# One mixed count tile, and one bias product instead of two, in a graph layer on one core

## The chip, the cores and the metric

The kernel runs on one core of a Trainium2 chip. The core has a matrix engine (PE, with its weight load shown apart as PEld), a vector engine (DVE), a scalar engine (ACT), a general engine (POOL) that also issues the indirect gathers, and a queue engine (SP) that issues most DMAs. [...] The metric is device time of one launch in microseconds (us), lower is better.

## The reference

One layer of a graph network with 12,500 nodes of 128 features and 400,000 edges sorted by target node. Each edge has a type, 0 or 1.

```python
Xs = X[src]
m_data = Xs @ W_data.T + b_data
m_ctrl = Xs @ W_control.T + b_control
msg = jnp.where((edge_types == 0)[:, None], m_data, m_ctrl)
agg = jax.ops.segment_sum(msg, dst, num_segments=X.shape[0])
out = agg + (X @ W_self.T + b_self)
x = _layernorm(x + jax.nn.relu(out), axis=-1)
```

Sums and products can be exchanged: for each node the source rows of its type-0 edges and of its type-1 edges are summed first, and the two sums are then multiplied with the two weight matrices. The bias of a type enters as often as the node has edges of that type, so the kernel also counts edges by type, and the biases are added as (count of type 0) x b_data + (count of type 1) x b_control + b_self.

## The kernel before, in words

**Work and windows.** The edges are cut into 25 groups (`NG`) of 500 target nodes each (`GN`). A group is worked in 4 or 5 windows; there are 107 windows (`pairs`), and the loop over `w` near the end of `short_path` writes one after the other. In a window most source rows come from a copy of the node table kept in SBUF (`x3`): one-hot matrices choose rows with PE (`pick`, L820), ACT casts the result from PSUM to bf16 (`emsg`, L834), and PE multiplies that with one-hot matrices of the target nodes (`sums`, L704), which DVE makes by comparing (`esel`, L504). Other rows are gathered from DRAM by POOL (L754). DVE also ranks the edges of later windows in the table (L504 to L690).

**Accumulators.** `sums` is added by DVE into `acc[g]` (L743), a tile of 128 partitions x 4 x 640 in f32, whose last axis runs over nodes. Parts 0 and 1 hold the two feature sums, transposed. Parts 2 and 3 hold the counts of type 0 and type 1. Counts come from PE products with `one_col` (L790, L842), whose first six columns are 1 and the others 0: so the same count lands on partitions 0 to 5 of parts 2 and 3 (and in the other quarters of 32 partitions, L842 adds the counts of three quarters of its chunks on 32 to 37, 64 to 69 and 96 to 101).

**Biases in bf16.** A bias is split into three bf16 parts whose sum is the f32 value (`bparts`, L414). Those nine rows go to DRAM (`b_parts`, one DMA, L422), and from there into the tile `bias` (`bias_rows`, L427): partitions 0 to 2 and 3 to 5 of each quarter carry the three parts of b_data (part 0 of `bias`) and of b_control (part 1). Partitions 6 to 8 of part 0 carry b_self, with a count of 1 put there from the start by `start1` (L319).

**Finishing.** When a group is complete, `finish_batch` (L911) handles up to four tiles of up to 125 nodes; there are 26 such batches with 101 tiles. Its units are `begin` (load of x), `counts`, `turn` (transpose x), one `product` a tile, `norm` and `write`. `counts` makes `cnt`, in bf16, for both types at once: ACT casts the two count parts, 128 x 1000 elements, to bf16 (L928); DVE then computes `cnt * left + acc` over the same elements (L929), where `left` is -1 on partitions 3 to 5 of a quarter and 0 elsewhere. So partitions 0 to 2 hold the rounded count and 3 to 5 what rounding left of it. `product` (L941) adds into one PSUM tile: x with the self weights, the two feature sums with their weights (these three in f32, two PE instructions each), and two bf16 products, `cnt` with `bias` for type 0 and for type 1. That is eight PE instructions a tile, all on L950.

**Order.** The units of a finished group are the list `rest` and are laid evenly over the part from 0.1 to 1 of the next window (`evenly(rest, 0.1)`, `merged`): `pass_on`, the finishing units, `begin_acc`. This is the written order; the framework then lays out each engine's order itself from the written order, the dependencies and its own estimate of durations, and sets the semaphore waits. The last group is split into two batches: the last one's `counts` is held back as `cnt2` and runs after the last accumulation, at the end of the kernel, followed by its products, `norm` and `write` (L1085, L1107).

The diff touches `short_path` with its inner functions `bparts`, `bias_rows` and `finish_batch`.

Of the kernel before, what the change touches and what calls it, by code (L numbers as in the profile page):

```python
# [17 lines left out]
P = 128  # L18
D = 128
# [4 lines left out]
NG = NC // GC  # L24
# [5 lines left out]
NE = 5  # L30
# [10 lines left out]
CAP = 32  # L41
# [109 lines left out]
def short_path(ctx, tc, const, ident, eps, wT, brow, bad, x, src, dst, etype, ws, bs, out):  # L151
    nc = tc.nc
    keep = ctx.enter_context(tc.tile_pool(name="keep", bufs=1))
    dram = ctx.enter_context(tc.tile_pool(name="dram", bufs=1, space=DRAM))
# [74 lines left out]
    for kind, i, c, _ in windows(0):  # L229
        if kind == "p":  # L230
            n = PL if i == NE - 1 else PB
            nc.sync.dma_start(
                out=near_i[i * PB:i * PB + n, :],
                in_=dst.rearrange("(o g e) -> o g e", o=1, g=NG)[:, :, c * P].to_broadcast([n, NG]),
# [49 lines left out]
    split_units, store_rows = split_x(pro.enter_context(tc.tile_pool(name="pro", bufs=4)))  # L284
    tmp = early.enter_context(tc.tile_pool(name="tmp", bufs=1))
    wn = tmp.tile([P, 3, D], FP, name="wn")
    bias = keep.tile([P, 2, D], BF, name="bias")
    nc.vector.memset(bias, 0.0)
    for i, (w, b) in enumerate(zip(ws, bs)):
        nc.sync.dma_start(out=wn[:, i, :], in_=w)  # L290
# [22 lines left out]
    lane_f = keep.tile([P, 1], FP, name="lane_f")  # L313
    nc.vector.tensor_copy(lane_f, iota([1], [[0, 1]], 0, 1, "i3"))
    zero = keep.tile([P, 1], FP, name="zero")
# [1 line left out]


    start1 = keep.tile([P, 1], FP, name="start1")  # L319
    nc.vector.tensor_scalar(start1, lane_f, 7.0, None, op0=OP.subtract)  # L320
    nc.vector.tensor_tensor(start1, start1, start1, op=OP.mult)
    nc.vector.tensor_single_scalar(start1, start1, 1.0, op=OP.is_le)
    left = keep.tile([P, 1], FP, name="left")
    quarter_i = iota([1], [[0, 1]], 0, 1, "i8")
    nc.vector.tensor_single_scalar(quarter_i, quarter_i, CAP - 1, op=OP.bitwise_and)
    nc.vector.tensor_scalar(left, quarter_i, 4.0, None, op0=OP.subtract)
    nc.vector.tensor_tensor(left, left, left, op=OP.mult)
    nc.vector.tensor_scalar(left, left, 1.0, -1.0, op0=OP.is_le, op1=OP.mult)
    blks = [keep.tile([P, NE, 2 * EC], BF, name=f"blk{k}") for k in range(3)]
    for t in blks:  # L330
        nc.vector.memset(t, -1.0)
# [13 lines left out]
        nc.vector.tensor_scalar(ltri[:, a, :], free[:, a, :], own_f[:, a:a + 1], None, op0=OP.is_gt)  # L345
    one_col = keep.tile([P, P], BF, name="one_col")
    nc.vector.memset(one_col, 0.0)
    nc.vector.memset(one_col[:, 0:6], 1.0)
    scale = tmp.tile([1, 2, P], BF, name="scale")
    nc.vector.memset(scale[:, 0, :], 128.0)  # L350
    nc.vector.memset(scale[:, 1, :], 1.0)
# [57 lines left out]
            nc.tensor.transpose(wps[:, i * D:(i + 1) * D], wn[:, i, :], ident)  # L409
        nc.scalar.copy(wT, wps[:, :3 * D].rearrange("p (i d) -> p i d", d=D))  # L410

    b_parts = dram.tile([3, 3, D], BF, name="b_parts")

    def bparts():  # L414

        part = tmp.tile([1, 3, 3, D], BF, name="part")
        rest = tmp.tile([1, 3, D], FP, name="rest")
        nc.vector.tensor_copy(part[:, 0], brow)
        nc.vector.tensor_tensor(rest, brow, part[:, 0], op=OP.subtract)
        nc.vector.tensor_copy(part[:, 1], rest)  # L420
        nc.vector.tensor_tensor(part[:, 2], rest, part[:, 1], op=OP.subtract)
        nc.sync.dma_start(  # L422
            out=b_parts.rearrange("j i d -> (j i d)").rearrange("(o e) -> o e", o=1),
            in_=part.rearrange("o j i d -> o (j i d)"),
        )

    def bias_rows():  # L427
        for at in [at + k for at in range(0, P, CAP) for k in (0, 3)]:
            nc.sync.dma_start(out=bias[at:at + 3, :, :], in_=b_parts[:, 0:2, :])
        nc.sync.dma_start(out=bias[6:9, 0, :], in_=b_parts[:, 2, :])  # L430


    codes = {}
# [468 lines left out]
    def finish(g, ks):  # L902
        full = P - 3
        tiles = []
        for k in ks:
            a, b = min(k * full, GN), min(k * full + full, GN + M0)
            a = M0 if g == 0 and k == 0 else a
            tiles.append((g * GN - M0 + a, a, b - a))
        return finish_batch(g, tiles)

    def finish_batch(g, tiles):  # L911
        s = {}
# [3 lines left out]
        def begin():  # L916
# [4 lines left out]
            for i, (n, _, rows) in enumerate(tiles):  # L921
                nc.sync.dma_start(out=s["xs"][:rows, i, :], in_=x[n:n + rows, :])

        def counts():
            a, b = tiles[0][1], tiles[-1][1] + tiles[-1][2]
            cnt = fp.tile([P, 2, 512], BF, name="cnt", bufs=1)
            s["cnt"] = cnt[:, :, :b - a]
            nc.scalar.copy(s["cnt"], acc[g][:, 2:4, a:b])  # L928
            nc.vector.scalar_tensor_tensor(  # L929
                s["cnt"], s["cnt"], left, acc[g][:, 2:4, a:b], op0=OP.mult, op1=OP.add  # L930
            )

        def turn():
            ps = side()
# [6 lines left out]
        def product(i):  # L941
            if i == 0:
                s["ph"] = side()
            _, c, rows = tiles[i]
            terms = [(s["xT"][:, i * P:i * P + rows], wT[:, 2, :])]
            terms += [(acc[g][:, t, c:c + rows], wT[:, t, :]) for t in range(2)]
            at = c - tiles[0][1]
            terms += [(s["cnt"][:, t, at:at + rows], bias[:, t, :]) for t in range(2)]
            for j, (left, right) in enumerate(terms):
                nc.tensor.matmul(  # L950
                    s["ph"][:rows, i * D:(i + 1) * D], left, right, start=(j == 0), stop=(j == len(terms) - 1)
                )
# [29 lines left out]
                )  # L982
                nc.sync.dma_start(out=out[n:n + r, :], in_=h[:r, i, :])

        return [begin, counts, turn] + [lambda i=i: product(i) for i in range(k)] + [norm, write]


    pairs = len(each_e)
# [77 lines left out]
    for w in range(pairs):  # L1066
        g, i = each_e[w]
        more = []
        if i == 1 and g + 1 < NG:
            more.append((0.1, lambda: prep_e(g + 1)))  # L1070
        if i == 1 and g + 1 < NG:
            more += evenly(prep_p(g + 1), 0.1, 0.7)
        if i == 3 and g + 2 < NG:
            load(g + 2, "e")
            load(g + 2, "p")
        tiled, begin = {}, []
        if w + 2 < pairs:
            tiled, begin = slots[w + 2]["tiled"], begun.pop(w + 2)
        elif w + 2 == pairs:
            tiled, begin = last_spares()  # L1080
        if w + 3 < pairs:
            more += [(0.55, lambda: [u() for u in begin_slots(w + 3)])]
        if w + 1 == pairs:
            closes = [at for at, _ in chunks[w]][-1 - of_p(NG - 1, NE - 1)]
            (xs, *most), (xs2, cnt2, turn2, *last) = (finish(NG - 1, soon[i]) for i in (NE - 2, NE - 1))  # L1085
            more += [(0.05, xs), (0.06, xs2), (0.98, turn2), (0.3, check_all)] + evenly(most, closes + 0.01, 0.97)
        units, ending = picked(w, tiled, ending, begin.pop(0)[1] if begin else None)
        merged(
            chunks.pop(w, []),
            units,  # L1090
            begin,
            pick_matrix(w + 1) if w + 1 < pairs else [],
            more,
            evenly(rest, 0.1),
        )
        slots.pop(w)
        rest = []
        for p in closed.pop(w, []):
            gp, ip = divmod(p, NE)
            if ip == NE - 1:  # L1100
                rest.append(lambda gp=gp: pass_on(gp))
                if gp < NG - 1:
                    rest += finish(gp, range(4))
                if gp + 2 < NG:
                    rest.append(lambda gp=gp: begin_acc(gp + 2))
    ending()
    for u in rest + [cnt2] + last:  # L1107
        u()


# [138 lines left out]
```

## Time and profile before

| | before |
|---|---|
| median of 3 runs | 1758.43 us (1756.07 to 1759.98) |
| the profiled execution, its own time | 1757.87 us |
| span of the profiled execution | 1756.1 us |
| PE busy in the span | 1615.3 us |
| DVE busy in the span | 1595.2 us |
| ACT busy in the span | 1229.2 us |
| POOL busy in the span | 1316.6 us |

How to read the views. A group row gives line, engine, operation, the written tile and what it reads, the shapes and the count; then busy time in us and the mean of one instruction in ns; then the idle time of that engine just before these instructions, with what ended most of it. The chain of waits is the work that ended last, followed back: a piece on it had nothing earlier to wait behind, and a piece off it had room. A timeline row is start, duration, engine, line, operation; in brackets stands an idle time before it and who ended it; "x2" means two merged instructions. Instructions of DVE and ACT overlap a little at their ends, so the distance from start to start is shorter than a duration. A piece marked "issue" is time in which the profile shows no wait. In the windows table each engine's busy time in a stretch stands with its number of instructions in brackets.

### The profile page before, as it was taken

To read this page: it belongs to the slowest core of one execution; us is meant where nothing else is said; L and a number is where in the kernel's file an instruction comes from. 1 tells how busy PE (TensorE), PEld (TensorE's weight loads), DVE (VectorE), ACT (ScalarE), POOL (GpSimd) and SP (SyncE) were. 2 spreads that over 40 slices of the span, in tenths; PEclk is the share of its full clock that TensorE was granted. 3 is DMA by queue.
4 is the path that set the end of the run, shared out by engine and by line. 5 is a ranking of instruction groups with operands and counts; after the bars stand their busy time and mean duration, and the time that the engine had idled before them with its cause. 6 is when DMAs were issued, how large, how long until landed. Compare 5 with 4: busy or idle time off the path is not lost.

```text
span 1756.1 us, 72083 instructions
## 1 busy us (share of the span) xinstructions
PE 1615.3 (92%) x29945; PEld 1311.7 (75%) x29945; DVE 1595.2 (91%) x3996; ACT 1229.2 (70%) x2249; POOL 1316.6 (75%) x1109
## 2 busy tenths in 40 slices
PE   0599999999999999999999999999999989999997
PEld 0377777777778777777877877777777777878786
DVE  8899999998999998999988999999999989999993
ACT  4577777767677667767766777776777766767675
POOL 0288877787777787877887877887877877777871
PEclk9999999999999999999999999999999999999999
DMA  8655454446454545444535454544454535544441
GB/s 237 209 165 160 128 158 136 147 125 199 115 164 134 159 125 179 143 152 127 166 119 164 150 164 133 164 122 147 160 159 135 158 108 162 167 139 141 151 139 41
DMA packets 190562, 261.28 MB, mean 149 GB/s; under 512 B 86437, under 2 KB 155983, under 8 KB 187152
## 3 DMA queue, kind: packets, MB, share of 16 engines
q1 hardware_dynamic: 126894, 148.02, 25.9%
q0 software_dynamic: 50704, 102.16, 20.8%
q10 hardware_dynamic: 12626, 6.40, 1.2%
q8 instruction: 236, 3.87, 0.9%
q14 instruction: 102, 0.84, 0.1%
HBM read 238.47 MB, written 18.00 MB: 146 GB/s over the span
## 4 chain that ended last, share of the span: by engine, by line
PE 48%; DVE 32%; issue 6%; DMA 6%; ACT 5%; DVEq 1%; POOL 1%; SPq 0%; POOLq 0%; ACTq 0%
PE sums L704 22%; PE got L820 15%; DVE esel L504 3%; PE side L950 3%; DVE pick L690 3%; PE sums L842 3%; DMA last<-rows,idx 3%; DVE rv L635 2%; ACT emsg L834 2%; DVE prod L598 2%; DVE prod L576 2%; PE side L584 2%; DVE acc L743 2%; PE side L647 2%; DVE ahead L594 2%
## 5 line engine op out<-in xcount | busy, mean ns | idle before, releaser
L754 POOL DMA_INDIRECT msg<-rows,pidx x985 | 1190.9, 1209 | 307.5 <-issue 118.9
L834 ACT CAST emsg<-got 128x768 bf16<-128x768 f32 (+1 forms) x1070 | 951.9, 930 | 303.9 <-PE got L820 289.8
L704 PE MATMUL sums<-esel,emsg 128*128 128x176 bf16 x7704 | 683.4, 240 | 0.0
L704 PEld LDWEIGHTS <-emsg 128*128 128x128 bf16 x7704 | 566.9, 98 | 68.7 <-issue 28.5
L820 PE MATMUL got<-x,pick 128*32 128x384 bf16 x10486 | 568.0, 330 | 21.9 <-DVE pick L690 14.7
L820 PEld LDWEIGHTS <-pick 128*32 128x32 bf16 x10486 | 239.2, 96 | 139.2 <-issue 20.6
L504 DVE TENSOR_TENSOR esel<-code_col,code 128x1760 bf16<-128x1760 bf16 x321 | 292.7, 912 | 13.6 <-PE sums L704 11.6
L798 POOL DMA_INDIRECT last<-rows,idx x107 | 122.0, 1141 | 106.0 <-DVE pick L690 63.7
L704 PE MATMUL sums<-psel,msg 128*128 128x48 bf16 x2955 | 184.2, 184 | 17.2 <-DVE acc L743 15.2
L842 PE MATMUL sums<-esel,one_col 128*32 128x176 bf16 x2675 | 193.7, 240 | 4.4 <-DVE acc L743 4.4
L704 PEld LDWEIGHTS <-msg 128*128 128x128 bf16 x2955 | 149.9, 97 | 36.2 <-issue 31.4
L842 PEld LDWEIGHTS <-one_col 128*32 128x32 bf16 x2675 | 111.9, 97 | 60.7 <-issue 4.1
L790 PE MATMUL sums<-psel,one_col 128*128 128x48 bf16 x985 | 150.2, 183 | 0.0
L743 DVE TENSOR_TENSOR acc<-acc,sums 128x352 f32 (+2 forms) x232 | 99.4, 430 | 40.4 <-PE sums L704 36.8
L504 DVE TENSOR_TENSOR O<-cell_col,blk 128x2000 bf16<-128x2000 bf16 x107 | 128.2, 1198 | 2.1 <-issue 2.1
L598 DVE TENSOR_TENSOR prod<-O,ahead 128x2000 bf16<-128x2000 bf16 x107 | 127.6, 1193 | 0.1
L690 DVE TENSOR_SCALAR pick<-pick,lane_f 128x3200 bf16<-128x3200 bf16 x107 | 113.2, 1058 | 0.0
L647 PE MATMUL side<-rv,O 128*128 128x64 bf16 x2140 | 83.3, 195 | 31.6 <-DVE rv L635 30.6
L647 PEld LDWEIGHTS <-O 128*128 128x128 bf16 x2140 | 78.7, 100 | 33.3 <-DVE rv L635 29.3
L594 DVE TENSOR_REDUCE ahead<-side 128x100 bf16<-128x500 f32 x107 | 72.2, 675 | 28.0 <-PE side L520 27.3
L790 PEld LDWEIGHTS <-one_col 128*128 128x128 bf16 x985 | 94.3, 96 | 0.0
L635 DVE TENSOR_TENSOR rv<-rm,vals 128x1280 bf16<-128x1280 bf16 x107 | 87.8, 821 | 0.3
(170 smaller groups left out, 1869.2 us busy)
## 6 DMA issues: line engine op xcount, KB each, us to landing
pick<-there SPq DMA_DIRECT2D x107, 800.0 KB
acc<-acc_start SPq DMA_DIRECT2D x23, 1280.0 KB
msg<-rows,pidx POOLq DMA_INDIRECT x985
rows<-x SPq DMA_DIRECT2D x6, 1344.0 KB
xs<-in_x_dram SPq DMA_DIRECT2D x99, 62.5 KB
out_dram<-h SPq DMA_DIRECT2D x99, 62.5 KB
xt<-in_x_dram ACTq DMA_DIRECT2D x6, 896.0 KB
there<-cell SPq DMA_DIRECT2D x107, 6.2 KB
```

What stands on the lines that cost most here:

```text
L504: nc.vector.tensor_tensor(sel.rearrange("p n (w t) -> p n w t", t=2), col[:rows].rearrange("p (o w t) -> p o w t", o=1, t=2).to_broadcast( ...
L598: nc.vector.tensor_tensor(prod, s["O"], ahead.rearrange("p (o j) -> p o j", o=1).to_broadcast([P, EC, NCELL]), op=OP.mult)
L635: placed[:] = [nc.vector.tensor_tensor(rv.rearrange("p c v (r t) -> p c v r t", t=2), rm.rearrange("p c (o r t) -> p c o r t", o=1, t=2).t ...
L647: nc.tensor.matmul(s["rk"][:m, :2 * CAP], s["held"][:, c * NCELL:c * NCELL + m], s["rv"][:, c].rearrange("p v r -> p (v r)"), start=(c == ...
L690: nc.vector.tensor_scalar(t, t, lane_f, None, op0=OP.is_equal)
L704: last = nc.tensor.matmul(out, msg[:, j * D:(j + 1) * D], sel, start=(start and j == 0), stop=stop, skip_group_check=True)
L743: added.append(nc.vector.tensor_add(win, win, ps[:, :4 * wide].rearrange("p (a w) -> p a w", w=wide)[:, :, :width]))
L754: return nc.gpsimd.indirect_dma_start(out=msg, out_offset=None, in_=rows3[:, :], in_offset=bass.IndirectOffsetOnAxis(ap=codes["p", g][0][: ...
L790: nc.tensor.matmul(cnt, one_col, sel, start=False, stop=(c == n - 1), skip_group_check=True)
L820: last = nc.tensor.matmul(ps[CAP * a:CAP * (a + 1), :], slots[w]["pick"][:, a * NQ + q, :], x3[:, 4 * q + a - a0].rearrange("p j d -> p (j ...
L834: nc.scalar.copy(msg[:, :n], ps[:, :n, :3 * D])
L842: nc.tensor.matmul(cells_of(s["ps"], EW, 1)[CAP * (q % 4):CAP * (q % 4 + 1), :], one_col[:, :CAP], s["sel"][q], start=(q < 4), stop=(q + 4 ...
```

## The change

Type 1's counts move to partitions of their own, so that one tile holds both types.

- `one_col` has twelve ones instead of six: each count lands on partitions 0 to 11 of a quarter.
- Four small [128, 1] tables replace one: `left` is now -1 on partitions 3 to 5 and 9 to 11, `second` is 1 on partitions 6 to 11, `plain` is 1 - `second`. `start1` moves to partitions 12 to 14.
- `bias` has one part instead of two: three parts of b_data on partitions 0 to 2 and 3 to 5, of b_control on 6 to 8 and 9 to 11, of b_self on 12 to 14 of the first quarter. `b_parts` is written in that order by five DMAs instead of one, and `bias` is read by four instead of nine.
- A new unit `mixed` comes before `counts`: ACT computes `mix = second * (counts of type 1)` in f32, 128 x 500, and DVE adds `plain * (counts of type 0)` to it. `counts` then does what it did, on `mix`: 128 x 500 instead of 128 x 1000 elements in both instructions.
- `product` has one bf16 product a tile in place of two.
- The held-back unit at the end becomes two, `mix2` and `cnt2`. The list `rest` has one unit more, so all its units stand a little elsewhere in the window.

```diff
-    bias = keep.tile([P, 2, D], BF, name="bias")
+    bias = keep.tile([P, D], BF, name="bias")
...
-    nc.vector.tensor_scalar(start1, lane_f, 7.0, None, op0=OP.subtract)
+    nc.vector.tensor_scalar(start1, lane_f, 13.0, None, op0=OP.subtract)
...
-    nc.vector.tensor_scalar(left, quarter_i, 4.0, None, op0=OP.subtract)
-    nc.vector.tensor_tensor(left, left, left, op=OP.mult)
-    nc.vector.tensor_scalar(left, left, 1.0, -1.0, op0=OP.is_le, op1=OP.mult)
+    kinds = [left] + [keep.tile([P, 1], FP, name=name) for name in ("left2", "second", "plain")]
+    for t, mid, wide in zip(kinds, (4.0, 10.0, 8.5), (1.5, 1.5, 7.0)):
+        nc.vector.tensor_scalar(t, quarter_i, mid, None, op0=OP.subtract)
+        nc.vector.tensor_tensor(t, t, t, op=OP.mult)
+        nc.vector.tensor_scalar(t, t, wide, -1.0 if t is not kinds[2] else 1.0, op0=OP.is_le, op1=OP.mult)
+    _, left2, second, plain = kinds
+    nc.vector.tensor_add(left, left, left2)
+    nc.vector.tensor_scalar(plain, second, -1.0, 1.0, op0=OP.mult, op1=OP.add)
...
-    nc.vector.memset(one_col[:, 0:6], 1.0)
+    nc.vector.memset(one_col[:, 0:12], 1.0)
...
-        nc.sync.dma_start(
-            out=b_parts.rearrange("j i d -> (j i d)").rearrange("(o e) -> o e", o=1),
-            in_=part.rearrange("o j i d -> o (j i d)"),
-        )
+        for i in range(3):
+            for k in range(2 if i < 2 else 1):
+                nc.sync.dma_start(
+                    out=b_parts[6 * i + 3 * k:6 * i + 3 * k + 3, :].rearrange("(o j) d -> o j d", o=1),
+                    in_=part[:, :, i, :],
+                )
...
-        for at in [at + k for at in range(0, P, CAP) for k in (0, 3)]:
-            nc.sync.dma_start(out=bias[at:at + 3, :, :], in_=b_parts[:, 0:2, :])
-        nc.sync.dma_start(out=bias[6:9, 0, :], in_=b_parts[:, 2, :])
+        for at in range(0, P, CAP):
+            n = 15 if at == 0 else 12
+            nc.sync.dma_start(out=bias[at:at + n, :], in_=b_parts[:n, :])
...
+        def mixed():
+            a, b = tiles[0][1], tiles[-1][1] + tiles[-1][2]
+            mix = fp.tile([P, 512], FP, name="mix", bufs=1)
+            s["mix"] = mix[:, :b - a]
+            nc.scalar.activation(s["mix"], acc[g][:, 3, a:b], AF.Identity, bias=zero, scale=second)
+            nc.vector.scalar_tensor_tensor(
+                s["mix"], acc[g][:, 2, a:b], plain, s["mix"], op0=OP.mult, op1=OP.add
+            )
+
         def counts():
-            a, b = tiles[0][1], tiles[-1][1] + tiles[-1][2]
-            cnt = fp.tile([P, 2, 512], BF, name="cnt", bufs=1)
-            s["cnt"] = cnt[:, :, :b - a]
-            nc.scalar.copy(s["cnt"], acc[g][:, 2:4, a:b])
-            nc.vector.scalar_tensor_tensor(
-                s["cnt"], s["cnt"], left, acc[g][:, 2:4, a:b], op0=OP.mult, op1=OP.add
-            )
+            cnt = fp.tile([P, 512], BF, name="cnt", bufs=1)
+            s["cnt"] = cnt[:, :s["mix"].shape[-1]]
+            nc.scalar.copy(s["cnt"], s["mix"])
+            nc.vector.scalar_tensor_tensor(s["cnt"], s["cnt"], left, s["mix"], op0=OP.mult, op1=OP.add)
...
-            terms += [(s["cnt"][:, t, at:at + rows], bias[:, t, :]) for t in range(2)]
+            terms.append((s["cnt"][:, at:at + rows], bias))
...
-        return [begin, counts, turn] + [lambda i=i: product(i) for i in range(k)] + [norm, write]
+        return [begin, mixed, counts, turn] + [lambda i=i: product(i) for i in range(k)] + [norm, write]
...
-    for u in rest + [cnt2] + last:
+    for u in rest + [mix2, cnt2] + last:
```

More of the change, by code (lines that the diff above doesn't have):

```diff
@@ L410, in places_and_weights @@
         nc.scalar.copy(wT, wps[:, :3 * D].rearrange("p (i d) -> p i d", d=D))
-    b_parts = dram.tile([3, 3, D], BF, name="b_parts")
+    b_parts = dram.tile([15, D], BF, name="b_parts")
     def bparts():
@@ L1084, in short_path @@
             closes = [at for at, _ in chunks[w]][-1 - of_p(NG - 1, NE - 1)]
-            (xs, *most), (xs2, cnt2, turn2, *last) = (finish(NG - 1, soon[i]) for i in (NE - 2, NE - 1))
+            (xs, *most), (xs2, mix2, cnt2, turn2, *last) = (finish(NG - 1, soon[i]) for i in (NE - 2, NE - 1))
             more += [(0.05, xs), (0.06, xs2), (0.98, turn2), (0.3, check_all)] + evenly(most, closes + 0.01, 0.97)
```

## The prediction

> **What bounds the kernel now.** First the page's head and the shares of the chain of waits.
>
> ```profile
> span 1756.1 us, 72083 instructions
> PE 1615.3 (92%) x29945; PEld 1311.7 (75%) x29945; DVE 1595.2 (91%) x3996; ACT 1229.2 (70%) x2249; POOL 1316.6 (75%) x1109
> PE 48%; DVE 32%; issue 6%; DMA 6%; ACT 5%; DVEq 1%; POOL 1%; SPq 0%; POOLq 0%; ACTq 0%
> ```
>
> PE and DVE are both nearly full and share the chain, so a microsecond saved on one or added to the other is worth a part of itself. The change touches the windows in which a group is finished, so next comes the table of stretches for three of them (the first row has none).
>
> ```profile
> core 0: us, PE busy (x) PEld busy (x) DVE busy (x) ACT busy (x) POOL busy (x), PEclk, DMA share, GB/s
> 1611.00:1627.00 16.00, 16.00 (x323) 13.15 (x320) 15.10 (x31) 11.84 (x19) 12.34 (x13) 1.00 0.47 151
> 1627.00:1643.00 16.00, 14.68 (x271) 11.62 (x269) 15.31 (x35) 11.12 (x24) 13.26 (x10) 1.00 0.37 112
> 350.00:366.00 16.00, 14.65 (x292) 11.72 (x293) 15.45 (x36) 12.18 (x25) 13.56 (x9) 1.00 0.42 136
> 1697.00:1713.00 16.00, 15.92 (x314) 13.14 (x304) 14.41 (x34) 13.08 (x21) 12.65 (x12) 1.00 0.50 164
> ```
>
> DVE has 0.6 to 1.6 us free of 16 there and PE 0.1 to 1.4, at the full granted clock; ACT has 3 to 5. Third, the chain itself: how often do the touched instructions lie on it?
>
> ```profile
> by line: PE sums L704 22.0%; PE got L820 15.4%; issue 6.4%; DVE esel L504 2.9%; PE side L950 2.7%; DVE pick L690 2.6%; PE sums L842 2.6%; DMA last<-rows,idx 2.6%; DVE rv L635 2.4%; ACT emsg L834 2.4%; DVE prod L598 2.2%; DVE prod L576 1.9%;
> 218.83 1.25 DVE cnt L929
> 1629.22 1.17 DVE cnt L929
> 289.35 0.93 ACT cnt L928
> 1697.82 1.03 ACT cnt L928
> 1716.08 0.80 PE side L950 x8
> 1717.93 0.85 PE side L950 x8
> ```
>
> The products have 2.7% of 1756 us = 47 us on the chain. Eight instructions, one tile, take 0.80 to 0.85 us, so 101 tiles take about 84: a weight of 47/84 = **0.55**. Of the 24 full-size DVE `cnt` instructions 11 lie whole on the chain (the first and last are shown) and 5 more with a fraction of 0.06 to 0.15 us that runs on as "issue" while DVE works at it: between 11/24 and 16/24, I take **0.55**. Of the 24 ACT casts 4 lie on it (first and last shown): **0.17**.
>
> **The change part by part.** *Removed: one bf16 product a tile.* Durations in group rows; the pitch of a product in a row of the timeline.
>
> ```profile
> L950 PE MATMUL side<-bias,cnt 128*125 128x128 bf16 x198 | 27.5, 221 | 0.4 <-DVE cnt L929 0.4
> 1739.13 0.28 PE L950 MATMUL side<-bias,cnt 128*125 128x128 bf16 x2
> ```
>
> Two products in a row take 0.28 us, one 0.22, so the second adds 0.06. 101 of them are 6.1 us of PE; at 0.55 that is **-3.4** (bounds 0, if DVE paces everywhere, and -6.1).
>
> *Replaced: one cast and one DVE instruction over 1000 columns by two of each over 500.*
>
> ```profile
> L928 ACT CAST cnt<-acc 128x1000 bf16<-128x1000 f32 x23 | 23.6, 1026 | 1.4 <-DVE acc L743 1.3
> L928 ACT CAST cnt<-acc 128x350 bf16<-128x350 f32 x1 | 0.5, 489 | 0.5 <-DVE acc L743 0.5
> L980 ACT ACTIVATE h<-h,nm,rs 125x128 f32<-125x128 f32 x99 | 41.0, 487 | 2.0 <-DVE nm L976 1.7 <-DVE O L504 0.2
> L725 ACT COPY acc<-start 128x500 f32<-128x500 f32 x1 | 0.6, 610 | 0.0
> L929 DVE SCALAR_TENSOR_TENSOR cnt<-cnt,left,acc 128x1000 bf16<-128x1000 bf16 x23 | 28.8, 1252 | 1.4 <-ACT emsg L834 0.9 <-issue 0.6
> L929 DVE SCALAR_TENSOR_TENSOR cnt<-cnt,left,acc 128x350 bf16<-128x350 bf16 x1 | 0.6, 586 | 0.6 <-ACT cnt L928 0.6
> 1697.82 1.03 ACT L928 CAST cnt<-acc 128x1000 bf16<-128x1000 f32 x1
> 1698.74 3.01 ACT L834 CAST emsg<-got 128x1152 bf16<-128x1152 f32 x3
> 1701.80 1.26 DVE L929 SCALAR_TENSOR_TENSOR cnt<-cnt,left,acc 128x1000 bf16<-128x1000 bf16 x1 [0.29 <-ACT emsg L834]
> 1702.97 0.36 DVE L605 TENSOR_TENSOR prod<-prod,eq 128x400 bf16<-128x400 bf16 x1
> ```
>
> DVE: 1252 against 586 ns over 650 columns is 1.02 ns a column and 0.23 us fixed, so 0.74 us at 500. The next instruction starts 1.17 us after a 1.26 us one, so each counts 0.08 less: 2 x 0.66 in place of 1.17 is +0.15 a batch, 24 batches +3.5 us, at 0.55 **+1.9** (0 to 3.5).
>
> [...]
>
> ACT: the plain cast at 500 columns is 0.61 us, by the copy of that very size and by the slope of the casts (537 ns over 650 columns, 0.83 ns each). The scaled one takes its scale and bias from [128, 1] tables, as L980 does: 0.487 us at 128 columns, with 372 x 0.83 ns more 0.79 us. A cast is followed after 0.92 of its 1.03 us, so each counts about 0.1 less: 0.69 + 0.51 in place of 0.92 is +0.28 a batch, +6.7 us in all, at 0.17 **+1.1** (0 to 6.7).
>
> *Added: a wait of ACT for DVE.* Before, work went once from ACT to DVE; now it goes ACT, DVE, ACT, DVE, and the second cast stands in ACT's queue until DVE has done `mix`. Behind it stand the `emsg` casts, for which PE's next row choice and sums wait. The trace has no such wait at this place; the nearest rows are small casts in ACT's queue that read what DVE made shortly before.
>
> ```profile
> L629 ACT CAST bits_b<-bits 128x24 bf16<-128x24 int32 x107 | 23.0, 215 | 52.8 <-DVE bits L627 47.6 <-DVE h L959 2.3 <-issue 1.5
> L489 ACT CAST blk<-parts 128x100 bf16<-128x100 int32 x25 | 6.9, 277 | 11.3 <-DVE eq L565 11.2
> L494 ACT CAST vals<-parts 128x200 bf16<-128x200 int32 x25 | 9.0, 362 | 10.7 <-DVE rv L635 10.5
> ```
>
> 47.6/107, 11.2/25 and 10.5/25 are 0.42 to 0.45 us a time; 24 times 0.44 is 10.6 us of idle ACT. What of it reaches the end lies between ACT's weight 0.17 (ACT has free time) and DVE's 0.55 (what ACT waits for is DVE); I take 0.35: **+3.7** (0 to 10.6). The opposite wait, DVE for ACT, ended an idle time of 0.29 us in the batch above, and L929 idles 1.4 us in 23 times, so I add nothing for it. The products start at 1716.08, 13 us after `cnt` is ready at 1703.06: a count chain some 2 us longer stays covered by that; without this cover its whole length would stall PE, as it does once, at the end.
>
> *The end.* There nothing covers the counts.
>
> ```profile
> 1743.73 0.52 DVE L743 TENSOR_TENSOR acc<-acc,sums 128x352 f32 x1 [1.25 <-PE sums L704]
> 1744.28 0.49 ACT L928 CAST cnt<-acc 128x350 bf16<-128x350 f32 x1 [0.51 <-DVE acc L743]
> 1744.81 0.59 DVE L929 SCALAR_TENSOR_TENSOR cnt<-cnt,left,acc 128x350 bf16<-128x350 bf16 x1 [0.56 <-ACT cnt L928]
> 1745.44 0.33 PE L950 MATMUL side<-bias,cnt 128*125 128x128 bf16 x2 [0.44 <-DVE cnt L929]
> ```
>
> Now 1744.28 to 1745.44, 1.16 us. Then, at 175 columns: scaled cast 0.53, DVE 0.41, cast 0.34, DVE 0.41 and four hand-overs of 0.04, together 1.85: +0.7, less two products of 0.06: **+0.6**.
>
> *The start.* Eleven more small DVE instructions on [128, 1] tables, and other DMAs.
>
> ```profile
> 13.10 0.14 DVE L322 TENSOR_SCALAR start<-start 128x1 f32<-128x1 f32 x1
> 13.17 0.14 DVE L328 TENSOR_SCALAR left<-left 128x1 f32<-128x1 f32 x1
> 67.01 0.36 SPq L659 DMA_DIRECT2D pick<-there  x1
> 67.83 3.64 SPq L429 DMA_DIRECT2D bias<-b_parts  x8
> 84.28 1.04 DVE L690 TENSOR_SCALAR pick<-pick,lane_f 128x3200 bf16<-128x3200 bf16 x1
> ```
>
> They follow each other at 0.07 us, 0.8 in all, where DVE works without a pause: **+0.7** (0 to 0.8). Four more stores of `b_parts` push SP's next issue, that of `pick` at 67.01, back by up to 4 x 0.45 (3.64/8) = 1.8 us; its reader starts at 84.28, so it is hidden, and would cost that 1.8 us otherwise. Loads of `bias` fall from nine to four, some 2 us of SP; its first use is in the first finished group, whole windows later. No gain.
>
> **Sum:** -3.4 + 1.9 + 1.1 + 3.7 + 0.6 + 0.7 = +4.6 us. The profiled execution took 1757.87 us, 1.8 more than its span, and 0.56 less than the median of 1758.43; so 1762.5 for it and **1763.0** for the median. All low bounds together give -5.5, all high ones +22: 1752.9 to 1780.6.
>
> **The rivals.** *PE sets the time:* the whole 6.1 us is gained, and what ACT and DVE get more falls into their idle time: -6.1 + 0.6 + 0.7, **1753.6**. For it: PE leads the chain, ACT has 3 to 5 us free a window. Against: DVE has 15.1 to 15.5 of 16 us in three of the four rows. This one is faster, where I forecast slower.
>
> *The wait is free:* the second cast is laid so late in ACT's order that DVE is always done. Sum without 3.7: +0.9, **1759.3**, no change to tell. For it: the engine orders are laid out from dependencies. Against: the three rows of waits above were laid out the same way.
>
> *The queue holds in full:* ACT waits with `emsg` casts behind it that PE needs at once, so all 10.6 us reach the end: **1769.9**. It decides where DVE runs behind ACT: at 1701.80 it took up what ACT had finished at 1698.85, 2.95 us later. Against: PE often has other products to do.
>
> *The products cost nothing:* PE has room that its busy time hides, so dropping one gains nothing: sum without -3.4, +8.0, **1766.4**. The weight load is busy only 75%. [...] Against: the products' 47 us on the chain.
>
> **How the numbers follow.** Forecast 0.40 (own range 1760 to 1768), PE sets the time 0.23, free wait 0.14, queue in full 0.15, products for nothing 0.08. About 0.2%, 3.5 us, can be told from no change: below 1754.9 and above 1761.9. Faster 0.23; same 0.14 and 0.06 of the forecast, 0.20; slower 0.34 + 0.15 + 0.08 = 0.57. The range follows the bounds; as every engine's order is laid out anew and PE's idle time in like windows differs by 1.3 us (16.00 against 14.68 busy), I put 3 us under the low end, and cut the top where all bad bounds must meet: 1750 to 1779.
>
> **What would show it.** Right: L950 with six f32 and one bf16 instruction a tile; DVE lines of the counts at 0.74 us each, ACT at 0.79 and 0.61; an idle time of some 0.4 us ahead of the second cast, ended by DVE `mix`; 1.8 us from the last accumulation to the last bias product. Wrong: fewer idle microseconds of PE ahead of L704 and L820 in finishing windows, the second cast without a wait, or a change in windows that finish nothing, which would be the new order and not a term of the sum.

## The result, and the profile after

| | before | changed |
|---|---|---|
| median, measured together | 1756.07 us (1752.09 to 1759.98, 7 runs) | 1766.11 us (1763.43 to 1767.95, 7 runs) |
| ratio to before | | 1.0050, 95% interval 1.0034 to 1.0066: +8.8 us (6.0 to 11.6) |
| profiled execution, its own time | 1757.87 us | 1763.63 us |
| span | 1756.1 us | 1761.8 us |

The changed kernel is slower. Here and below, a difference in us is a ratio's distance from 1 times 1757 us; a difference between two kernels that were both measured against before is the difference of their ratios, and its interval comes from both.

First the head of the changed kernel's page and the shares of its chain of waits.

```profile
span 1761.8 us, 71944 instructions
PE 1609.5 (91%) x29844; PEld 1307.4 (74%) x29844; DVE 1597.3 (91%) x4030; ACT 1236.7 (70%) x2275; POOL 1323.2 (75%) x1109
PE 46%; DVE 33%; DMA 8%; issue 6%; ACT 5%; DVEq 1%; POOL 0%; SPq 0%; ACTq 0%; POOLq 0%
```

PE lost 5.8 us of work (1615.3 before), nearly the 6.1 of the removed products, while DVE gained 2.1 and ACT 7.5. The span still grew by 5.7, so PE stands idle longer, 152.3 us in place of 140.8 (span less busy time). On the chain PE fell from 48 to 46%, and DVE and DMA rose, DMA from 6 to 8%. That rise is not the gather of spare rows spoken of below, which has 2.6% before and 2.7% now; new in the page's list is a load of edge sources (`esrc`) with 2%, and why is open.

Next the touched instructions, grouped by line and shape: busy time, mean ns, idle time ahead of them and what ended it.

```profile
L963 PE MATMUL side<-bias,cnt 128*125 128x128 bf16 x99 | 21.8, 220 | 1.1 <-DVE cnt L944 1.1
L935 ACT ACTIVATE mix<-acc,zero,second 128x500 f32<-128x500 f32 x23 | 18.5, 805 | 1.4 <-DVE acc L750 1.3
L936 DVE SCALAR_TENSOR_TENSOR mix<-acc,plain,mix 128x500 f32<-128x500 f32 x23 | 16.8, 730 | 2.5 <-ACT mix L935 1.1 <-ACT emsg L841 0.9 <-issue 0.6
L944 DVE SCALAR_TENSOR_TENSOR cnt<-cnt,left,mix 128x500 bf16<-128x500 bf16 x23 | 16.7, 726 | 0.1
L943 ACT CAST cnt<-mix 128x500 bf16<-128x500 f32 x23 | 14.0, 610 | 4.9 <-DVE mix L936 4.6
```

One bf16 product a tile is left, and the four durations are 0.81, 0.73, 0.61 and 0.73 us where 0.79, 0.74, 0.61 and 0.74 were forecast. The added wait is there: 4.6 us of idle ACT ahead of L943 were ended by DVE's `mix`. One place where it occurs, in the timeline:

```profile
910.22 0.74 DVE L936 SCALAR_TENSOR_TENSOR mix<-acc,plain,mix 128x500 f32<-128x500 f32 x1 [0.29 <-ACT emsg L841]
910.99 0.61 ACT L943 CAST cnt<-mix 128x500 bf16<-128x500 f32 x1 [0.91 <-DVE mix L936]
911.50 0.79 ACT L841 CAST emsg<-got 128x768 bf16<-128x768 f32 x1
```

DVE takes up `mix` only at 910.22, ACT stands idle for 0.91 us, and the `emsg` cast that PE needs follows behind. But this is one of few: the list of waits (us in total, times, longest) has it 8 times among 26 batches.

```profile
PE sums L711 <- DMA last<-rows,idx: 22.8, 10, 5.9
...
ACT cnt L943 <- DVE mix L936: 5.0, 8, 0.9
...
DVE mix L936 <- ACT mix L935: 2.2, 4, 0.8
```

The first row holds the larger difference. Before, the same row of that list was this:

```profile
PE sums L704 <- DMA last<-rows,idx: 15.2, 11, 4.5
```

So 7.6 us more of idle PE are spent waiting for `last`, the spare rows that POOL gathers at the end of a window. The change touches neither that gather nor its DMA; it only comes at another moment against PE. These sums, from one trace each, do not rank the kernels: the kernel with only an empty unit, below, is faster than before and has more of this wait.

Three of the stretches read before, 6 us later in the span, look much as they did:

```profile
1617.00:1633.00 16.00, 16.00 (x324) 13.23 (x322) 15.14 (x31) 11.67 (x20) 12.36 (x12) 1.00 0.47 150
1633.00:1649.00 16.00, 14.57 (x278) 11.79 (x276) 15.38 (x35) 12.16 (x26) 13.19 (x10) 1.00 0.38 111
1703.00:1719.00 16.00, 15.67 (x306) 13.01 (x299) 14.29 (x35) 13.28 (x21) 12.83 (x11) 1.00 0.51 161
```

PE is busy 16.00, 14.57 and 15.67 of 16 us, where it was 16.00, 14.68 and 15.92 before. But they cannot stand for all finishing windows: no bias product of the changed kernel lies in them, and only those of one tile did before. Over the first 24 batches together, in the 30 us from 2 us ahead of the counts' first ACT instruction (L928 before, L935 now), PE idles 29.6 us before and 37.7 now; in the 40 us from that instruction on it is 48.9 and 51.4. So how much of the 11.5 us of added idle time falls beside the finishing units is not settled. The longest single wait for the spare rows is the one near 900 us, just ahead of a batch whose counts begin at 904.97. First the kernel before, then the changed one, each in the timeline (POOL's issue of the gather, for the changed kernel with the gather issued ahead of it, and PE's first product with it) and in the table of stretches (PE, PEld, DVE, ACT, POOL busy, then the granted clock, DMA share, GB/s).

```profile
894.92 3.01 POOL L798 DMA_INDIRECT last<-rows,idx  x1 [0.30 <-ACT emsg L834]
900.09 0.40 PE L704 MATMUL sums<-esel,last 128*128 128x176 bf16 x3 [3.04 <-DMA last<-rows,idx]
897.00:900.10 3.10, 0.06 (x2) 0.02 (x2) 0.14 (x2) 0.00 (x0) 2.49 (x3) 1.00 0.43 98
900.10:903.50 3.40, 3.40 (x62) 2.61 (x63) 2.85 (x6) 2.78 (x7) 2.61 (x3) 1.00 0.72 260
```

```profile
894.47 3.04 POOL L761 DMA_INDIRECT msg<-rows,pidx  x1 [0.30 <-PE got L827]
897.82 0.91 POOL L805 DMA_INDIRECT last<-rows,idx  x1 [0.30 <-issue]
902.49 0.62 PE L711 MATMUL sums<-esel,last 128*128 128x176 bf16 x3 [5.90 <-DMA last<-rows,idx]
896.60:902.50 5.90, 0.01 (x1) 0.02 (x2) 0.09 (x1) 0.00 (x0) 4.67 (x5) 0.73 0.58 201
902.50:905.90 3.40, 3.40 (x43) 1.77 (x43) 1.98 (x3) 2.11 (x6) 2.50 (x3) 0.50 0.29 77
```

PE was out of work at 897.05 before and at 896.59 now (the start of its product less the idle time), but POOL now has one more gather of `msg`, of 3.04 us, in front, and the gather of `last` is issued at 897.82 instead of 894.92. That issue took 3.01 us before and takes 0.91 now, so it ends only 0.80 us later; the rows then let PE start 3.76 us after it, and not 2.16. So of the 2.86 us by which the gap grows, from 3.04 to 5.90, PE's earlier stop makes 0.46, the later issue 0.80 and the longer landing 1.60. After the gap PE runs 3.4 us at a granted clock of 0.50, with 43 instructions where 62 ran before. Such stretches lower the mean granted clock of the whole span, which is 0.991 against 0.995.

At the end of the kernel nothing covers the counts:

```profile
1749.69 0.53 ACT L935 ACTIVATE mix<-acc,zero,second 128x175 f32<-128x175 f32 x1 [0.52 <-DVE acc L750]
1750.25 0.40 DVE L936 SCALAR_TENSOR_TENSOR mix<-acc,plain,mix 128x175 f32<-128x175 f32 x1 [0.60 <-ACT mix L935]
1750.69 0.34 ACT L943 CAST cnt<-mix 128x175 bf16<-128x175 f32 x1 [0.47 <-DVE mix L936]
1751.06 0.40 DVE L944 SCALAR_TENSOR_TENSOR cnt<-cnt,left,mix 128x175 bf16<-128x175 bf16 x1 [0.41 <-ACT cnt L943]
1751.52 0.27 PE L963 MATMUL side<-bias,cnt 128*125 128x128 bf16 x1 [1.11 <-DVE cnt L944]
```

From 1749.69 to 1751.52 are 1.83 us, where 1.85 were forecast and 1.16 stood before.

And the start, in the timeline of before and then of the changed kernel (SP's issue of the second load of targets, and DVE's first work on it):

```profile
7.15 0.33 SPq L201 DMA_DIRECT2D edst<-in_dst_dram  x1
...
9.04 0.22 DVE L360 TENSOR_SCALAR halves<-first_e 1x125 int32<-1x125 int32 x1 [6.03 <-DMA edst<-in_dst_dram]
```

```profile
8.00 0.33 SPq L201 DMA_DIRECT2D edst<-in_dst_dram  x1
...
10.10 0.21 DVE L365 TENSOR_SCALAR halves<-first_e 1x125 int32<-1x125 int32 x1 [7.14 <-DMA edst<-in_dst_dram]
```

Already here, ahead of every small instruction that was added, the changed kernel is 1.06 us late.

### The profile page after: what moved, and what is told of

The parts are those of the page before. It is cut to its first block, busy times and chain, and to the rows that moved or that the text cites. A ratio compares the mean times of both kernels' runs of the same rounds, so it can differ in the third digit from the quotient of the medians.

```text
span 1761.8 us, 71944 instructions
## 1 busy us (share of the span) xinstructions
PE 1609.5 (91%) x29844; PEld 1307.4 (74%) x29844; DVE 1597.3 (91%) x4030; ACT 1236.7 (70%) x2275; POOL 1323.2 (75%) x1109
## 4 chain that ended last, share of the span: by engine, by line
PE 46%; DVE 33%; DMA 8%; issue 6%; ACT 5%; DVEq 1%; POOL 0%; SPq 0%; ACTq 0%; POOLq 0%
PE sums L711 21%; PE got L827 15%; DVE esel L511 3%; DVE pick L697 3%; DMA last<-rows,idx 3%; ACT emsg L841 2%; DVE rv L642 2%; PE sums L849 2%; PE side L963 2%; DVE prod L605 2%; DMA esrc<-in_src_dram 2%; DVE prod L583 2%; DVE acc L750 2%; PE side L591 2%; DVE ahead L601 2%
## 5 line engine op out<-in xcount | busy, mean ns | idle before, releaser
L511 DVE TENSOR_TENSOR esel<-code_col,code 128x1760 bf16<-128x1760 bf16 x321 | 292.3, 911 | 10.2 <-PE sums L711 8.6
```

Source lines behind the costliest of these rows:

```text
L511: nc.vector.tensor_tensor(sel.rearrange("p n (w t) -> p n w t", t=2), col[:rows].rearrange("p (o w t) -> p o w t", o=1, t=2).to_broadcast( ...
```

## The experiments

All were timed in five rounds beside the kernel before on the same chip. "Against the changed kernel" means the difference of the two ratios; the changed kernel's own ratio is the one above, measured apart from these rounds.

**One product dropped** from the kernel before.

```diff
-            terms += [(s["cnt"][:, t, at:at + rows], bias[:, t, :]) for t in range(2)]
+            terms += [(s["cnt"][:, t, at:at + rows], bias[:, t, :]) for t in range(1)]
```

> The kernel before, without the bias product of type 1 (101 bf16 products fewer; the biases of type 1 are left out of the result). Nothing else moves. Sum of terms: -3.4 us against the kernel before (6.1 us of PE at a weight of 0.55). PE sets the time: -6.1. Products cost nothing: within 1 us of before. Order theory (the engines' order is laid out anew and PE waits for the gathered spare rows at other places): anything between -5 and +5, with the waits of PE for `last` going along with it.

Measured 1751.03 against 1755.99 us, ratio 0.9976 (0.9960 to 0.9993): **-4.2 us** (-7.0 to -1.2). The product is worth something on the path, and the interval holds both the -3.4 of the sum and the whole 6.1.

**A second product put back into the changed kernel**, with zeros for weights.

```diff
+    none = keep.tile([P, D], BF, name="none")
+    nc.vector.memset(none, 0.0)
...
-            terms.append((s["cnt"][:, at:at + rows], bias))
+            terms += [(s["cnt"][:, at:at + rows], bias), (s["cnt"][:, at:at + rows], none)]
```

> The changed kernel with a second bf16 product a tile whose right side is a tile of zeros: the 101 products are back, all else is as changed. Sum of terms: 3.4 us slower than the changed kernel, about 13 us slower than before. Products cost nothing: as the changed kernel, 10 us slower than before.

1772.59 us, ratio 1.0095 (1.0077 to 1.0113): **+7.9** (3.7 to 12.1) against the changed kernel. In its group rows the added products last as long as the others:

```profile
L965 PE MATMUL side<-none,cnt 128*125 128x128 bf16 x99 | 21.9, 222 | 0.0
L965 PE MATMUL side<-bias,cnt 128*125 128x128 bf16 x99 | 21.8, 220 | 1.1 <-DVE cnt L946 1.1
```

The pitch of two products gives 6.1 us of PE for all of them, and about that much, or all of it, reaches the end. That the products cost nothing is ruled out. Not all of the 7.9 need be theirs: this kernel also has one more tile at the start, and in its trace DVE's first `pick` instruction starts at 70.21 us, 1.27 later than in the changed kernel.

**The wait taken away**: the second cast reads the count in the accumulator instead of `mix`, so it waits for nothing of DVE's.

```diff
-            nc.scalar.copy(s["cnt"], s["mix"])
+            nc.scalar.copy(s["cnt"], acc[g][:, 2, tiles[0][1]:tiles[-1][1] + tiles[-1][2]])
```

> The changed kernel, with the second cast reading the count part of type 0 in the accumulator instead of `mix`: same instructions and sizes, but ACT has no wait for DVE in `counts` (the rounding of type 1's counts is left out of the result). Wait theory: 3.7 us faster than the changed kernel (up to 5, which is the idle time that its profile shows ahead of this cast), so about 6 us slower than before. Order theory: no nearer to before by more than 2 us for this reason, or moved by a change in PE's waits for `last`.

1759.19 us, ratio 1.0024 (1.0006 to 1.0041): **-4.6** (-8.8 to -0.4) against the changed kernel. In its list of waits no idle time of ACT ahead of the cast is left, and PE's wait for the spare rows is shorter too:

```profile
PE sums L711 <- DMA last<-rows,idx: 14.9, 4, 6.2
```

The long gap near 900 us does not come from the wait, though. Here, too, POOL issues a `msg` gather of 3.04 us ahead of the gather of `last`, and PE stands still even longer:

```profile
904.72 0.62 PE L711 MATMUL sums<-esel,last 128*128 128x176 bf16 x3 [6.21 <-DMA last<-rows,idx]
```

**Only the shift of places**: the kernel before with one empty unit in the list.

```diff
-        return [begin, counts, turn] + [lambda i=i: product(i) for i in range(k)] + [norm, write]
+        return [begin, lambda: None, counts, turn] + [lambda i=i: product(i) for i in range(k)] + [norm, write]
...
```

> The kernel before with one empty unit in the list of finishing units, where the change puts `mixed`: the same instructions, but the finishing units stand a little elsewhere in the window, as in the changed kernel. Sum of terms: as before, within 1 us, since no term is in it. Order theory: a good part of the 10 us, 4 us or more slower than before.

1752.18 us, ratio 0.9980 (0.9967 to 0.9993): **-3.5** (-5.8 to -1.2). A list with one more place, and no other difference, is faster: a shift like the one in the change is a gain here, and has nothing to do with biases. In its list of waits PE waits longer for the spare rows than in the kernel before (15.2), although the kernel is faster:

```profile
PE sums L704 <- DMA last<-rows,idx: 20.7, 15, 3.7
```

**The shift taken back**, in the changed kernel: `mix` is made together with the load of x, and the other units stand where they stood before.

```diff
-                    rest += finish(gp, range(4))
+                    first, mixes, *others = finish(gp, range(4))
+                    rest += [lambda first=first, mixes=mixes: (first(), mixes())] + others
```

> The changed kernel with mix made together with the load of x, so that counts, turn, products, norm and write stand where they stood before; mix and the second cast stay a unit apart, so the wait stays short. If the shift of the units by one place is worth the -3.5 that it was worth in the kernel before, this kernel takes +3.5 against the changed one (about +12 against before). If the shift is worth nothing here: 0 (+9). If the shift is why the changed kernel loses (its gathers come late): -5 or more.

1768.83 us, ratio 1.0078 (1.0055 to 1.0100): **+4.9** (0 to 9.8) against the changed kernel, at the edge of what can be told, and on the side of the first theory. So the shift is not why the change loses; it seems to hide a part of the loss.

**Both halves of the counts in one unit**, in the changed kernel, so that the second cast is written right behind `mix`.

```diff
-        return [begin, mixed, counts, turn] + [lambda i=i: product(i) for i in range(k)] + [norm, write]
+        return [begin, lambda: (mixed(), counts()), turn] + [lambda i=i: product(i) for i in range(k)] + [norm, write]
...
```

> The changed kernel with `mixed` and `counts` in one unit, so that the finishing units stand where they stood before the change; the same instructions. The empty unit alone made the kernel before 3.5 us faster; if that gain is in the changed kernel too, this one is some 3.5 us slower than the changed kernel. Wait theory adds to that: the second cast is written right behind `mixed`, its wait for DVE is as long or longer, 0 to 5 us more. So 13 to 18 us slower than before. If the position does not matter, 10 us slower than before.

1772.35 us, ratio 1.0104 (1.0083 to 1.0125): +18.3 against before, **+9.5** (4.9 to 14.1) against the changed kernel. The size came out just above the upper end, the reason did not. Its list of waits:

```profile
ACT cnt L943 <- DVE mix L936: 5.0, 8, 0.9
```

That is the very row of the changed kernel: the wait did not grow. Of the 9.5 the shift that is lost with the unit would explain some 5, by the run before this one; the rest is no larger than the error of either, and stays open.

**Only the small tables**, in the kernel before: `left`, `left2`, `second` and `plain` are made at the start as in the changed kernel, and only `left` is used (its new values on partitions 9 to 11 meet counts of zero).

```diff
-    nc.vector.tensor_scalar(left, quarter_i, 4.0, None, op0=OP.subtract)
...
+    kinds = [left] + [keep.tile([P, 1], FP, name=name) for name in ("left2", "second", "plain")]
...
+    nc.vector.tensor_scalar(plain, second, -1.0, 1.0, op0=OP.mult, op1=OP.add)
```

> The kernel before with the four small tables made as in the change (eleven more small DVE instructions at the start, whose results are not used except `left`, the same where it matters); batches, products and DMAs as before. Sum of terms: +0.7 us against before. Order theory: up to 3 us either way from a new order behind them.

1759.01 against 1756.36 us, ratio 1.0027 (1.0008 to 1.0046): **+4.7** (1.4 to 8.1), and not 0.7.

**The tables computed later**, in the changed kernel.

```diff
...
+    def tables():
+        for t, mid, wide in zip(kinds, (4.0, 10.0, 8.5), (1.5, 1.5, 7.0)):
...
     bias_rows()
+    tables()
```

> The changed kernel with its small tables computed after the first window's choices are begun, with the loads of bias, and not at the start. Theory 1, the instructions at the start cost what the tables alone showed (+4.7, of which the first choice starts 2.7 us later): -2.7 to -4.7 against the changed kernel, and the first choice starts at 67 us. Theory 2, as predicted, 0.07 us each: -0.7. Theory 3, the start is later for another cause that goes with the tables (their places in memory, which stay): no change, the first choice at 69 to 70.

1766.40 us, ratio 1.0061 (1.0040 to 1.0081): +1.9 (-2.7 to +6.5) against the changed kernel, no difference. But the edit did not do what it was made for:

```profile
15.31 0.20 DVE L332 TENSOR_SCALAR left<-i 128x1 f32<-128x1 int32 x2
```

The small instructions start at 15.31 us, only 1.75 later than in the changed kernel (13.56) and long before the first window's choices, since the framework lays out each engine's order itself. So this run does not tell the instructions from what goes with them, such as the places of the tiles in memory.

**Only the halving**, in the kernel before: two casts of 500 columns and two DVE instructions of 500, one a type.

```diff
-            nc.scalar.copy(s["cnt"], acc[g][:, 2:4, a:b])
-            nc.vector.scalar_tensor_tensor(
-                s["cnt"], s["cnt"], left, acc[g][:, 2:4, a:b], op0=OP.mult, op1=OP.add
-            )
+            for t in range(2):
+                nc.scalar.copy(s["cnt"][:, t], acc[g][:, 2 + t, a:b])
+            for t in range(2):
+                nc.vector.scalar_tensor_tensor(
+                    s["cnt"][:, t], s["cnt"][:, t], left, acc[g][:, 2 + t, a:b], op0=OP.mult, op1=OP.add
+                )
```

> The kernel before with the cast of 1000 columns written as two of 500, one a type, and the DVE instruction likewise; nothing between them crosses the engines anew, both products and all positions stay. By the terms of the sum DVE gives +1.9 (0 to 3.5) and ACT, now two plain casts of 0.61 us less 0.1 each against 0.92, 24 x 0.10 x 0.17 = +0.4, at the end +0.2: about +2.5 against before. Rival: the four runs so far leave +10.9 for the halving with what goes with it; if the halving by itself is that, this kernel takes +9 to +11. Within +-2 of no change says that the rest of the +10.9 is not in the halving.

1758.63 against 1754.86 us, ratio 1.0023 (1.0005 to 1.0041): **+4.0** (0.9 to 7.2). The rival of +9 to +11 is out; the +2.5 of the sum of terms is inside. Its groups have the durations that the sum used:

```profile
L931 DVE SCALAR_TENSOR_TENSOR cnt<-cnt,left,acc 128x500 bf16<-128x500 bf16 x46 | 33.4, 730 | 2.1 <-ACT emsg L834 1.2 <-ACT cnt L929 0.7 <-issue 0.3
L929 ACT CAST cnt<-acc 128x500 bf16<-128x500 f32 x46 | 27.1, 611 | 1.4 <-DVE acc L743 1.3
```

**Without the rounding step, mixed**: in the changed kernel ACT scales and DVE writes `cnt` in bf16 at once; the second pair of instructions is gone. bf16 holds whole numbers up to 256, so this computes the same as long as no node has more edges of a type (the mean is 16 a type). The counts then stand on three partitions a type, 0 to 2 and 6 to 8.

```diff
...
-                s["mix"], acc[g][:, 2, a:b], plain, s["mix"], op0=OP.mult, op1=OP.add
+                s["cnt"], acc[g][:, 2, a:b], plain, s["mix"], op0=OP.mult, op1=OP.add
...
-            nc.scalar.copy(s["cnt"], s["mix"])
-            nc.vector.scalar_tensor_tensor(s["cnt"], s["cnt"], left, s["mix"], op0=OP.mult, op1=OP.add)
+            pass
```

> The changed kernel without the rounding step: DVE writes `mix` in bf16 and the second cast and the second DVE instruction are gone; the rows that carried what rounding left get no count, so counts over 256 of one type would be rounded. One product a tile, one hand-over from ACT to DVE. Sum of terms against the changed kernel: DVE 24 x 0.65 x 0.55 = -8.6, ACT 24 x 0.51 x 0.17 = -2.1, the wait -4.6 as the run without it showed: -15, so 5 us faster than before. If the waits and not the instructions are the loss: about -5 against the changed kernel, 5 us slower than before.

1749.68 us, ratio 0.9973 (0.9963 to 0.9983): **-4.7** (-6.5 to -3.0) against before, and -13.5 (-16.8 to -10.2) against the changed kernel, where the terms gave -15.

**Without the rounding step, and nothing mixed**: the kernel before without its DVE instruction L929, the counts on three partitions of a quarter, both products kept; the same bound of 256.

```diff
             nc.scalar.copy(s["cnt"], acc[g][:, 2:4, a:b])
-            nc.vector.scalar_tensor_tensor(
-                s["cnt"], s["cnt"], left, acc[g][:, 2:4, a:b], op0=OP.mult, op1=OP.add
-            )
...
-    nc.vector.memset(one_col[:, 0:6], 1.0)
+    nc.vector.memset(one_col[:, 0:3], 1.0)
```

> The kernel before without its DVE instruction in `counts` and with the counts on three partitions instead of six (counts over 256 of one type would be rounded); two products a tile and one ACT cast of 1000 columns stay. Sum of terms: 24 x 1.17 x 0.55 = -15 us against before. If DVE's time at this place is hidden: -3 or less.

1737.19 us, ratio 0.9904 (0.9879 to 0.9929): **-16.9** (-21.3 to -12.5). The rounding step costs two to four times what the second product does. Its busy times:

```profile
PE 1609.8 (93%) x29945; PEld 1312.9 (76%) x29945; DVE 1570.8 (90%) x3970; ACT 1228.9 (71%) x2249; POOL 1288.8 (74%) x1109
```

DVE has 24.4 us less work than the 1595.2 of before, so a microsecond of it weighs 16.9/24.4 = 0.7 here; the chain gave 0.55. The mean granted clock of these six runs is also higher, 0.9967, and what of the 16.9 goes with that is not parted from DVE's work.

**The same with one empty unit** in the list, as in the run of the shift alone.

> The kernel before without its second instruction of the counts, the counts on three partitions of a quarter (-17 against before), with one empty unit in the list of the finishing units (-3.5). If the two add: -20. If the shift is worth something only beside long DVE work in the same place: -17. Above -14 the shift is not a gain in itself but chance of the order.

1733.33 against 1754.86 us, ratio 0.9881 (0.9861 to 0.9902): **-20.9** (-24.4 to -17.2), the fastest kernel of the study. Against the run before this one the empty unit is worth -4.0 (-9.7 to +1.7): the two gains may add, but this alone does not tell a gain from none.

## Why the prediction came out as it did

The forecast was 1763.0 us, 4.6 above the median shown; measured were +8.8 (6.0 to 11.6). The side was right, and the durations and the end were right to a few hundredths of a microsecond. By its own steps:

- **The removed product, -3.4.** -4.2 in the kernel before, -7.9 in the changed one. Both intervals hold the whole 6.1 us, and only the first holds the 3.4, so the weight of 0.55 from the chain was too small rather than too large. The rival *the products cost nothing* pointed to the weight load's busy share of 75%; that this share tells how much room PE has was not shown, and both runs show a cost.
- **The halving, +1.9 and +1.1.** +4.0 (0.9 to 7.2) for two plain casts and two DVE instructions: in agreement.
- **The wait, +3.7.** -4.6 (-8.8 to -0.4) when it is taken away. The worth came out right by luck, from two factors that were off in opposite directions: 24 waits of 0.44 us, 10.6 in all, were forecast and 8 with 5.0 us were there; by the middle of the interval nearly all of that, and not 0.35, reached the end. The chain of before showed that ACT is rarely on the path; why so large a part of its wait should reach the end is not shown.
- **The end, +0.6.** 1.83 us against 1.85.
- **The start, +0.7.** This step failed in its size: the tables alone cost +4.7 (1.4 to 8.1). "They follow each other at 0.07 us" held, but DVE's first work on loaded data is already 1.06 us late, and the added instructions come after it. The forecast priced the new instructions one by one and had no term for a later first load. In the traces the first `pick` instruction of DVE (L690 before) starts at 66.7 to 67.3 us in the six kernels without the tables and at 68.9 to 71.0 in the eight with them; for the changed kernel that is 2.0 us, and where the rest of the 4.7 arises is open.
- **The places in the list.** They were given no term, only 3 us at the low end of the range. Alone the shift is worth -3.5. That it nearly cancels what was missed at the start is luck.

Together: product -6.1 (the mean of -4.2 and -7.9), halving +4.0, wait +4.6, end +0.6, start +4.7, places -3.5 make +4.3. Against the measured +8.8 the 4.5 that remain are within the error of a sum of six such measurements (about 7 us, from their half-intervals added as squares), so the runs don't show a further term, and don't exclude one. The forecast of +4.6 thus stands near the sum of the parts, and half of what was measured. Of its signs of being wrong two showed in part: 18 of the 26 second casts had no wait, and the start, which finishes nothing, changed.

Of the rivals, *PE sets the time* had the product's price right and the cover wrong: ACT's and DVE's added work did not fall into idle time. *The queue holds in full* is out in its size, as only 8 of 26 casts waited, 5.0 us and not 10.6; that what there is of the wait reaches the end in full, as it had it, fits the -4.6. *The wait is free* and *the products cost nothing* fell with the runs that took away the one and doubled the other. The second of them has the number that came nearest to the measured median, 1766.4 against 1766.1, so the time alone would have spoken for the wrong rival.

What the forecast had no word for is a part of how the loss shows: in places where the spare rows reach PE late, and in a granted clock of 0.50 at the gaps of 3.04 us (306 us) and 5.90 us (902 us). The way by which the wait costs its 4.6 us stays open. PE's wait for the spare rows falls from 22.8 to 14.9 us without it, and the mean granted clock of the runs rises from 0.9899 to 0.9925; but the longest of these waits stays (6.21 us), and with the empty unit alone PE waits longer for the spare rows (20.7) than before in a faster kernel.

## What to carry to other kernels

Before two operations are merged to save a third, price the rearrangement at the engines that must do it: here the second product cost 4 to 8 us, the step that fed both products 17. Where the written order is spread evenly over a window, try the order alone (an empty unit) before putting a gain or a loss down to an edit. Weights from a chain of waits gave here the side of a term and its size within a factor of about two, no better.

## What the runs showed of the hardware that was not expected

- **A lower mean clock goes with a longer time, but does not set it.** Over the seven timed runs of the changed kernel the mean granted clock averages 0.9899, over 65 runs of the kernel before, measured beside the experiments, 0.9941. 0.0042 of 1756 us is 7.4 us of clock, most of the loss if PE could have used it all. In those 65 runs the 17 at 0.993 average 1757.2 us and the 10 at 0.996 average 1753.7. It is not the only way to lose time: the kernel with only the tables added has a mean of 0.9940 and is 4.7 us slower, and the mixed one without the rounding step has 0.9925 and is 4.7 us faster.
- **A gap need not be long for half clock.** In the changed kernel a gap of 3.04 us, as long as the one of before at 897 us that left the clock at 1.00, goes with half clock:

```profile
306.15 0.62 PE L711 MATMUL sums<-esel,last 128*128 128x176 bf16 x3 [3.04 <-DMA last<-rows,idx]
306.10:309.50 3.40, 3.35 (x46) 2.20 (x47) 2.44 (x4) 1.85 (x6) 2.76 (x3) 0.50 0.34 93
```

  The 3.40 us of the rows above is the length of the stretch that was looked at. By the trace's records of the granted clock it stood at 0.50 for 6.8 us at each of these two places of the changed kernel (305.3 to 312.2 us, from 0.8 us before the product with the spare rows, and 899.3 to 906.1 us), for 3.4 us at three others (from 387.3, 1329.3 and 1442.0 us), and from 1752.6 us on, after the last products. A gap of 3.04 us went with half clock here once and once did not, so the length of a gap alone does not decide; what else does was not shown.
- **Eleven tiny instructions and three tiles went with later first loads.** SP's issue of the second load of targets came at 8.00 us instead of 7.15, with the same instructions ahead of it on that queue; it comes at 7.13 to 7.34 in the six traces without the tables and at 7.69 to 8.97 in the eight with them. Why is open; computing the tables later did not tell, as they were laid at the start again.
- **Single runs of the same kernel spread by 1.0%** (1747.4 to 1764.6 us in those 65 runs of before), so that a term of 4 us needs some ten runs of both kernels to be seen.
